# Attention's whole-array matmuls in one stretch, and its turned weights moved in 1280-byte pieces in a diagonal order

## The chip, the cores and the metric

The kernel runs on one core of a Trainium2 chip. The metric is the device time of one execution in microseconds (us). A core has five engines, each with a queue of its own that runs in order: TensorE (PE in the profile; its weight loads are PEld), VectorE (DVE), ScalarE (ACT), GpSimd (POOL) and SyncE, which here only issues DMA transfers (SPq). The transfers run on 16 DMA engines. SBUF is the on-chip memory of 128 partitions; PSUM holds the results of TensorE in 8 banks of 128x512 float32 numbers.

## The reference

The input x has 16 sequences of 512 tokens of width 256, all in float32. Three layers follow one another, each with a layer norm ahead and a residual around it: half a slot-and-expert layer, causal attention, and half a slot-and-expert layer again. The change is in attention alone:

```python
q = x @ Wq + bq;  k, v = split(x @ Wkv + bkv)   # 16 heads of 64
q, k = rope(q), rope(k)
probs = softmax(where(causal, q @ k.T / 8, -inf))
out = concat_heads(probs @ v) @ Wo + bo
x = x + out
```

## The kernel before

The first layer, attention and the last layer run one after another. Attention is cut into 64 units: each of the 16 sequences in 4 groups of 4 heads. A loop over u (from -2 to 63, near line 1100) runs one *turn* per step, and in a turn different units are at different stages: unit u has its weighted sums and output projection, unit u+1 its turning and its values, unit u+2 its scores and exponentials, unit u+3 its queries and keys. All engines run their instructions in the order in which the loop writes them out (manual_schedule), so the order of the lines is the order of each queue.

The stages, by the tile names in the profile:

- **p_av** (sums, L1054): probabilities times values, in tiles 128\*64 of the array, two heads side by side. It reads prT, the turned probabilities, and so waits for their transfers.
- **p_as** (scores, L956): queries times keys in tiles 32\*128, four heads at a time. A unit's rows come in four blocks: `scores((3,))` is the longest block of 512 columns; `scores((2,))` and `scores((1, 0))` are the others.
- **p_v** (values, L920), **p_q** and **p_k** (queries and keys, L898), **p_ay** (output projection, `leave`, L1070) and **p_ahT** (turning of a new sequence's x, `width`, L883, in every fourth turn) use the whole array, 128\*128.

After the scores VectorE adds the mask and takes the extremum (L974), ScalarE takes the exponential (L978), VectorE the reciprocal of the sum (L983), and GpSimd multiplies (L986, `scaled`). VectorE also rotates queries and keys (L904) with GpSimd (L909, L910), adds p_ay to x (L1076) and takes the statistics of finished tokens (`token_stats`, L198, L199).

The probabilities have to be turned (keys on partitions) for the sums. `turn_most`, `turn_corner` and `turn_rest` make seven VectorE transposes of 32x32 blocks into the tile sq (L1001). Then `move` (L1024) lets SyncE issue 16 transfers from sq to prT, each from one group of 32 partitions to another; both sides are 5120 contiguous bytes in each partition, and the outer loop is over the target group. The tiles sq and prT have one buffer each. PSUM's banks are handed out in turn: a new tile takes the bank of the tile eight before it, and waits until that has been read.

In a turn before, TensorE's order is p_av, (p_ahT), p_as of block 3, p_v, p_q, p_k, p_v, p_as of the other blocks, p_ay. `leave` returns a function, `added`, with p_ay's addition and the transfer of finished rows to memory; it is kept in the list `gone` and runs in the next turn, behind `move`. `spread` (ScalarE's square root for the layer norm) stands ahead of the second scores' exponentials, and `pair_rstd`, seven more square roots for the last layer, at the end of turn 60.

Of the kernel before, what the change touches and what calls it, by code (L numbers as in the profile page):

```python
# [9 lines left out]
F32 = mybir.dt.float32  # L10
AF = mybir.ActivationFunctionType
ALU = mybir.AluOpType
# [3 lines left out]
P = 128  # L16
NB, S, D = 16, 512, 256
# [3 lines left out]
PB = 2  # L21
# [13 lines left out]
HG = 4  # L35
NHG = AH // HG
SQ = 32
NSQ = P // SQ
# [9 lines left out]
def macaron_kernel(ctx: ExitStack, tc: tile.TileContext, a: dict, out: bass.AP):  # L48
# [144 lines left out]
    def token_stats(b, t):  # L193
        g = b // PB
        if b % PB == 0 and t == 0:
            mvs[g] = small.tile([P, PB * NT, 2], F32, tag=f"mv{g}", name=f"mv{g}", bufs=2)
        st = small.tile([P, 6], F32, tag="bnst", name=f"bnst{b}_{t}")
        nc.vector.bn_stats(st, xs[b][:, t, :])  # L198
        nc.vector.bn_aggr(mvs[g][:, (b % PB) * NT + t, :], st)  # L199
# [644 lines left out]
    def attention(qp, wq, wk, wv, wo, cos, sin, row):  # L844
# [14 lines left out]
        def scales(g, std):  # L859

            n = PB * NT
            rstds[g] = small.tile([P, n], F32, tag=f"rstd{g}", name=f"rstd{g}", bufs=1)
            nc.vector.reciprocal(rstds[g], std)
            pair_shift(g)
# [13 lines left out]
        def width(b):  # L878
            hTs[b] = qp.tile([P, NC, S], F32, tag="hT", name=f"ahT{b}", bufs=2)
            for c in range(NC):  # L880
                pt = ps(f"p_ahT{b}_{c}")
                for t in range(NT):
                    nc.tensor.transpose(pt[:, t * P:(t + 1) * P], hs[b][t // 2][:, t % 2, c * P:(c + 1) * P], ident)  # L883
                nc.scalar.copy(hTs[b][:, c, :], pt)  # L884
# [27 lines left out]
        def values(u, t0):  # L912
            b, hg = units[u]
            if t0 == 0:
                pool, tag, bufs = (ap, "v", 1) if u + 1 < nu else (qp, "hT", 2)
                vs[u] = pool.tile([P, NT, HG * DQ], F32, tag=tag, name=f"v{b}_{hg}", bufs=bufs)
            pv = ps(f"p_v{b}_{hg}_{t0}")
            for t in range(2):
                for k in range(NC):
                    nc.tensor.matmul(pv[:, t * 256:(t + 1) * 256], hTs[b][:, k, (t0 + t) * P:(t0 + t + 1) * P],  # L920
                                     wv[:, k, hg * HG * DQ:(hg + 1) * HG * DQ],
                                     start=(k == 0), stop=(k == NC - 1))
            nc.scalar.copy(vs[u][:, t0:t0 + 2, :].rearrange("p t d -> p (t d)"), pv)  # L923
# [8 lines left out]
        class Weights:  # L932
# [56 lines left out]
            def turn(self, which, heads, of, src, dst):  # L989

                if heads[0] == 0 and which == 0 and len(of) == 2:
                    self.sq = ap.tile([P, NSQ, HG, blocks * SQ], F32, tag="sq", name=f"sq{self.nm}")
                pr = self.pr[which]

                def view(x, at, dims):
                    return bass.AP(x.tensor, x.offset + at, [list(x.ap[0])] + [[s, n] for s, n in dims if n > 1])
                j, nh = heads
                step = (7, 3)[which] * P  # L1000
                nc.vector.transpose(  # L1001
                    view(self.sq, j * blocks * SQ + dst[0] * SQ,
                         [(blocks * SQ, nh)] + [(s * SQ, n) for s, (_, n) in zip(dst[1:], of)]
                         + [(HG * blocks * SQ, NSQ), (1, SQ)]),
                    view(pr, j * step + src * P,
                         [(step, nh)] + [(s * P, n) for s, n in of] + [(SQ, NSQ), (1, SQ)]))

# [10 lines left out]
            def move(self):  # L1018


                prT = prTs[self.u] = ap.tile([P, NSQ, HG, blocks * SQ], F32, tag="prT", name=f"prT{self.nm}")
                for k in range(NSQ):
                    for q in range(NSQ):
                        nc.sync.dma_start(prT[k * SQ:(k + 1) * SQ, q, :, :], self.sq[q * SQ:(q + 1) * SQ, k, :, :])  # L1024

            def turn_at_once(self):

# [37 lines left out]
        def leave(u, t0):  # L1065
            b, hg = units[u]
            py = ps(f"p_ay{b}_{hg}_{t0}")
            for t in range(2):
                for pair in range(HG // 2):
                    nc.tensor.matmul(py[:, t * D:(t + 1) * D], oTs[u][:, pair, (t0 + t) * P:(t0 + t + 1) * P],  # L1070
                                     wo[:, hg * (HG // 2) + pair, :],
                                     start=(pair == 0), stop=(pair == HG // 2 - 1))

            def added():
                xt = xs[b][:, t0:t0 + 2, :]
                nc.vector.tensor_tensor(xt, py.rearrange("p (t d) -> p t d", t=2), xt, ALU.add)  # L1076
                if hg == NHG - 1:
                    nc.sync.dma_start(xout[b][:, t0:t0 + 2, :], xt)
            return added

# [14 lines left out]
        seen = 2 * NHG  # L1097
        with tc.manual_schedule(engines={mybir.EngineType.DVE, mybir.EngineType.Activation,
                                         mybir.EngineType.Pool, mybir.EngineType.SP}):
            gone = []  # L1100
            for u in range(-2, nu):
                new = ws[u + 2] = Weights(u + 2) if u + 2 < nu else None
                qk = queries_keys(u + 3)
                old = ws.get(u + 1)
                fresh = u + 3 < nu and units[u + 3][1] == 0
                if fresh:
                    enter(units[u + 3][0])
                if u + 2 == nu:
                    old.scaled((1, 0))
                    values(u + 1, 0)  # L1110
                    values(u + 1, 2)
                if u >= 0:
                    sums(u, 0)
                    sums(u, 1)
                if old and u + 2 == nu:
                    old.turn_at_once()
                elif old:
                    old.turn_most(0)
                    old.scaled((1, 0), slice(0, HG // 2))
                    old.turn_most(1)  # L1120
                    old.scaled((1, 0), slice(HG // 2, HG))
                    old.turn_most(2)
                    old.turn_most(3)
                    old.turn_corner()
                    old.turn_rest()
                    old.move()
                for one in gone:
                    one()
                if fresh:
                    with_bias(units[u + 3][0])  # L1130
                if u + 4 in stds:
                    scales((u + 4) // (PB * NHG), stds.pop(u + 4))
                if fresh:
                    width(units[u + 3][0])
                if new:
                    new.scores((3,))
                    new.exps((3,))

                for at in range(seen, min(u + 13, NB * NHG)):
                    token_stats(*divmod(at, NHG))  # L1140
                seen = max(seen, u + 13)
                if u >= NHG + 1:
                    token_stats(*divmod(u - NHG - 1, NHG))
                if new:
                    new.scaled((3,))
                if 0 <= u + 1 < nu - 1:
                    values(u + 1, 0)
                for one in qk:
                    one()
                if 0 <= u + 1 < nu - 1:  # L1150
                    values(u + 1, 2)
                if 0 <= u + 5 < nu and (u + 5) % (PB * NHG) == 0:
                    stds[u + 5] = spread((u + 5) // (PB * NHG))
                if new:
                    new.scores((2,))
                    new.scores((1, 0))
                    new.exps((2,))
                    new.exps((1, 0), lambda: new.scaled((2,)))

                if u == nu - NHG:  # L1160
                    for g in range(NB // PB - 1):
                        pair_rstd(g)
                if u == nu - 1:
                    for g in range(PB):
                        entered[g] = xs[g]
                        for t in range(NT):
                            i = (g % PB) * NT + t
                            nc.vector.tensor_scalar(xs[g][:, t, :], xs[g][:, t, :], mvs[g // PB][:, i, 0:1],
                                                    rstds[g // PB][:, i:i + 1], ALU.subtract, ALU.mult)
                gone = [leave(u, 0), leave(u, 2)] if u >= 0 else []  # L1170
                if u >= nu - 2:
                    for one in gone:
                        one()
                    gone = []
            token_stats(NB - 2, NT - 1)
        yield
    with ExitStack() as es:
# [53 lines left out]
```

## Time and profile before

| what | us |
|---|---|
| median of 3 runs | 2330.49 |
| lowest and highest of the runs | 2329.22, 2330.73 |
| the profiled execution | 2332.58 |
| its span on the profile's page | 2330.9 |
| attention's first and last sums start (timeline of TensorE) | 447.5, 1937.2 |
| an ordinary turn, from p_av to p_av | 23.36 |

The page gives each engine's busy time and its share of the span. A timeline row gives start, duration, engine, line, operation, tiles and a count of merged instructions, and in brackets an idle time before it and what ended it. A tile's name carries its purpose: `p_av<-prT,v` writes p_av and reads prT and v. For matmuls the array tile is given (32\*128 is 32 rows by 128 columns). Each float32 matmul of the code appears as two records. A row of the windows view gives, for its stretch, each engine's busy time (and its number of instructions), the granted clock of TensorE, the busy share of the DMA engines and GB/s.

### The profile page before, as it was taken

The numbers are of one execution on the slowest core, as the hardware profiler recorded it, in microseconds if no ns is written. First come the engines' busy times: TensorE is split into PE (matmuls) and PEld (weight loads), VectorE is DVE, ScalarE is ACT, GpSimd is POOL, SyncE is SP. The second block draws the span as 40 slices with busy tenths as digits, with TensorE's granted clock in tenths as the row PEclk, the third lists the DMA queues.
The fourth block names the chain that finished last, engine by engine and source line by source line (L and its number), as shares of the span: only waits on it lengthen the run. The fifth ranks groups of instructions, "written<-read, shape, count | busy, mean of one in ns | idle before, by whom it ended". The sixth has DMA issues, their size and how long they took to land. (4 is left out here: it accounts for less than half of the span.)

```text
span 2330.9 us, 42260 instructions
## 1 busy us (share of the span) xinstructions
PE 2285.0 (98%) x14496; PEld 1453.5 (62%) x14496; DVE 1754.1 (75%) x4658; ACT 1123.7 (48%) x3046; POOL 1061.9 (46%) x1692
## 2 busy tenths in 40 slices
PE   7999999999999999999999999999999999999999
PEld 5665588465656565565656565655656566664588
DVE  6742397888888888898888888888888874442387
ACT  4743243455455545554645545554555454542233
POOL 2210054565555565655656555556565541210043
PEclk9999999999999999999999999999999999999999
DMA  6839851345555464645455555546464543839834
GB/s 223 252 124 406 321 137 46 85 97 129 107 119 126 103 134 93 142 103 129 107 123 113 126 111 116 129 100 137 91 140 105 127 110 96 241 115 405 329 115 140
DMA packets 159710, 346.77 MB, mean 149 GB/s; under 512 B 38980, under 2 KB 98952, under 8 KB 151304
## 3 DMA queue, kind: packets, MB, share of 16 engines
q1 hardware_dynamic: 158636, 343.27, 55.4%
q8 instruction: 115, 1.88, 0.4%
q14 instruction: 99, 0.81, 0.1%
q10 hardware_dynamic: 860, 0.81, 0.1%
HBM read 148.95 MB, written 29.88 MB: 77 GB/s over the span
## 5 line engine op out<-in xcount | busy, mean ns | idle before, releaser
L986 POOL TENSOR_SCALAR pr<-pr,ars 128x512 f32<-128x512 f32 (+3 forms) x1024 | 522.1, 532 | 631.5 <-DVE ars L983 631.5
L978 ACT ACTIVATE pr<-pr,amn 128x512 f32<-128x512 f32 (+3 forms) x1024 | 560.5, 549 | 268.4 <-DVE amn L974 268.2
L974 DVE CUSTOM_DVE_ANT_0 pr<-p_as,causal 128x512 f32<-128x512 f32 (+3 forms) x1024 | 433.9, 484 | 96.6 <-PE p_as L956 96.6
L1001 DVE STREAM_TRANSPOSE sq<-pr 128x768 f32<-128x768 f32 x441 | 379.0, 906 | 0.2 <-issue 0.2
L956 PE MATMUL p_as<-k,q 32*128 32x128 f32 (+3 forms) x4096 | 325.3, 445 | 7.1 <-DVE k L904 3.4
L1054 PE MATMUL p_av<-prT,v 128*64 128x512 f32 (+3 forms) x2048 | 292.1, 438 | 1.9 <-DVE amn L974 1.9
L956 PEld LDWEIGHTS p_as<-k,q 32*128 32x128 f32 x4096 | 192.4, 186 | 107.4 <-issue 49.6
L920 PEld LDWEIGHTS p_v<-wv,ahT 128*128 128x128 f32 x1024 | 189.4, 190 | 97.4 <-issue 75.6
L920 PE MATMUL p_v<-wv,ahT 128*128 128x256 f32 x1024 | 248.1, 385 | 0.0
L923 ACT COPY v<-p_v 128x512 f32<-128x512 f32 x128 | 73.3, 574 | 353.1 <-PE p_v L920 353.1
L1070 PE MATMUL p_ay<-wo,aoT 128*128 128x256 f32 x1024 | 240.5, 388 | 0.2 <-ACT aoT L1061 0.2
L1054 PEld LDWEIGHTS p_av<-prT,v 128*64 128x64 f32 x2048 | 138.1, 138 | 161.7 <-issue 136.5
L898 PE MATMUL p_k<-ahT,wk 128*128 128x512 f32 x512 | 230.6, 592 | 0.4 <-DVE amn L974 0.4
L898 PE MATMUL p_q<-ahT,wq 128*128 128x512 f32 x512 | 230.5, 593 | 0.2 <-ACT ahT L884 0.2
L1070 PEld LDWEIGHTS p_ay<-wo,aoT 128*128 128x128 f32 x1024 | 190.8, 191 | 32.0 <-ACT aoT L1061 0.6
L978 ACT ACTIVATION_READ_ACCUMULATOR pr<-pr,amn 128x1 f32 x1024 | 191.7, 187 | 0.0
L898 PEld LDWEIGHTS p_k<-ahT,wk 128*128 128x128 f32 x512 | 97.2, 190 | 122.7 <-issue 110.5
L898 PEld LDWEIGHTS p_q<-ahT,wq 128*128 128x128 f32 x512 | 97.1, 190 | 95.8 <-issue 85.4
L717 POOL TENSOR_TENSOR kbd<-kT,own 128x256 f32<-128x256 f32 x32 | 19.7, 619 | 267.4 <-DVE kT L680 235.5
L1061 ACT ACTIVATE aoT<-p_av,bcol 128x512 f32<-128x512 f32 x128 | 87.4, 684 | 108.9 <-PE p_av L1054 108.9
L770 PE MATMUL p_cy<-vw,catT 128*128 128x256 f32 x512 | 120.8, 379 | 0.0
L548 PE MATMUL p_ds<-hT,qk 128*128 128x512 f32 x256 | 118.3, 606 | 2.3 <-ACT hT L241 2.3
(167 smaller groups left out, 3252.0 us busy)
## 6 DMA issues: line engine op xcount, KB each, us to landing
prT<-sq SPq DMA_DIRECT2D x1008, 160.0 KB
w<-in_e_W_dram SPq DMA_DIRECT2D x64, 1024.0 KB
w<-in_e_Wg_dram SPq DMA_DIRECT2D x32, 1024.0 KB
out_dram<-x SPq DMA_DIRECT2D x64, 256.0 KB
awaya<-sqa SPq DMA_DIRECT2D x25, 512.0 KB
atT<-awaya SPq DMA_DIRECT2D x100, 128.0 KB
xl<-in_attn_x_dram SPq DMA_DIRECT2D x16, 512.0 KB
xl<-out_dram SPq DMA_DIRECT2D x16, 512.0 KB
```

Source lines behind the costliest of these rows:

```text
L548: nc.tensor.matmul(psc, qk[:, k, c * P:(c + 1) * P], hT[:, k, :], start=(k == 0), stop=(k == NC - 1))
L770: nc.tensor.matmul(py[:, t * D:(t + 1) * D], atT[:, c, t * P:(t + 1) * P], vws[b][:, c, :], start=(c == 0), stop=(c == NC - 1))
L898: nc.tensor.matmul(pq, self.w[:, k, at:at + P], hTs[self.b][:, k, :], start=(k == 0), stop=(k == NC - 1))
L920: nc.tensor.matmul(pv[:, t * 256:(t + 1) * 256], hTs[b][:, k, (t0 + t) * P:(t0 + t + 1) * P], wv[:, k, hg * HG * DQ:(hg + 1) * HG * DQ], s ...
L956: nc.tensor.matmul(banks[j][:, at:at + w], q[n][j * 32:(j + 1) * 32, i * P:(i + 1) * P], k[n][j * 32:(j + 1) * 32, :w], start=(n == 0), st ...
L974: nc.vector.tensor_tensor_reduce(out=self.at(i, j), in0=banks[j][:, at:at + w], in1=causal[:, S - w:], scale=-1.0 / math.sqrt(DQ), scalar= ...
L978: nc.scalar.activation(self.at(i, j), self.at(i, j), AF.Exp, bias=self.mn[:, i, j:j + 1], scale=-1.0, accum_out=self.rs[:, i, j:j + 1])
L986: nc.gpsimd.tensor_scalar(self.at(i, j), self.at(i, j), self.rs[:, i, j:j + 1], 1.0, ALU.mult, ALU.mult)
L1001: nc.vector.transpose(view(self.sq, j * blocks * SQ + dst[0] * SQ, [(blocks * SQ, nh)] + [(s * SQ, n) for s, (_, n) in zip(dst[1:], of)] + ...
L1054: nc.tensor.matmul(po[j * DQ:(j + 1) * DQ, :].rearrange("d (a f) -> d a f", a=NSQ)[:, :, t * SQ:], vs[u][:, t, head * DQ:(head + 1) * DQ], ...
L1061: nc.scalar.activation(oTs[u][:, pair, :].rearrange("d (i a y) -> d a i y", i=NT, a=NSQ), po.rearrange("d (a i y) -> d a i y", i=NT, a=NSQ ...
L1070: nc.tensor.matmul(py[:, t * D:(t + 1) * D], oTs[u][:, pair, (t0 + t) * P:(t0 + t + 1) * P], wo[:, hg * (HG // 2) + pair, :], start=(pair ...
```

## The change

The tile sq has its dimensions in another order, `[P, HG, NSQ, ...]` for `[P, NSQ, HG, ...]`, so that VectorE's transposes write the same 32-number runs to other places, and each transfer reads four pieces of 1280 bytes where it read one of 5120. The target side is as before. The order of the 16 transfers is diagonal: the target group k runs fastest, and the source group is (k + n) mod 4.

TensorE's order in a turn becomes p_av, p_as of block 3, p_v, (p_ahT), p_v, p_q, p_k, p_ay, p_as of the other blocks. `leave` makes its addition at once, and `gone` is no more. On ScalarE the copies of p_v stand ahead of the first scores' exponentials, and `spread` behind them. On GpSimd the rotations stand ahead of `scaled((3,))`, and the bias on x (`with_bias`) behind it. On VectorE the first scores' mask work follows `move`, then one token's statistics, the rotations, the additions of p_ay, another token's statistics, and the second scores. `pair_rstd` runs in turn 61, behind that turn's transposes. The counts and forms of the compute instructions are the same.

```diff
-                    self.sq = ap.tile([P, NSQ, HG, blocks * SQ], F32, tag="sq", ...)
+                    self.sq = ap.tile([P, HG, NSQ, blocks * SQ], F32, tag="sq", ...)
...
-                for k in range(NSQ):
-                    for q in range(NSQ):
-                        nc.sync.dma_start(prT[k * SQ:(k + 1) * SQ, q, :, :], self.sq[q * SQ:(q + 1) * SQ, k, :, :])
+                for n in range(NSQ):
+                    for k in range(NSQ):
+                        q = (k + n) % NSQ
+                        nc.sync.dma_start(prT[k * SQ:(k + 1) * SQ, q, :, :], self.sq[q * SQ:(q + 1) * SQ, :, k, :])
...
-            def added():
-                xt = xs[b][:, t0:t0 + 2, :]
-                nc.vector.tensor_tensor(xt, py..., xt, ALU.add)
-                if hg == NHG - 1:
-                    nc.sync.dma_start(xout[b][:, t0:t0 + 2, :], xt)
-            return added
+            xt = xs[b][:, t0:t0 + 2, :]
+            nc.vector.tensor_tensor(xt, py..., xt, ALU.add)
+            if hg == NHG - 1:
+                nc.sync.dma_start(xout[b][:, t0:t0 + 2, :], xt)
...
                     old.move()
-                for one in gone:
+                if u + 4 in stds:
+                    scales((u + 4) // (PB * NHG), stds.pop(u + 4))
+                if new:
+                    new.scores((3,))
+                if 0 <= u + 1 < nu - 1:
+                    values(u + 1, 0)
+                if fresh:
+                    width(units[u + 3][0])
+                if 0 <= u + 1 < nu - 1:
+                    values(u + 1, 2)
+                if new:
+                    new.exps((3,))
+                for one in stats:
+                    token_stats(*one)
+                for one in qk:
                     one()
+                if new:
+                    new.scaled((3,))
                 if fresh:
                     with_bias(units[u + 3][0])
-                if u + 4 in stds:
-                    scales((u + 4) // (PB * NHG), stds.pop(u + 4))
-                if fresh:
-                    width(units[u + 3][0])
-                if new:
-                    new.scores((3,))
-                    new.exps((3,))
...
-                if new:
-                    new.scaled((3,))
-                if 0 <= u + 1 < nu - 1:
-                    values(u + 1, 0)
-                for one in qk:
-                    one()
-                if 0 <= u + 1 < nu - 1:
-                    values(u + 1, 2)
                 if 0 <= u + 5 < nu and (u + 5) % (PB * NHG) == 0:
                     stds[u + 5] = spread((u + 5) // (PB * NHG))
-                if new:
-                    new.scores((2,))
-                    new.scores((1, 0))
-                    new.exps((2,))
-                    new.exps((1, 0), lambda: new.scaled((2,)))
-                if u == nu - NHG:
+                if u == nu - NHG + 1:
                     for g in range(NB // PB - 1):
                         pair_rstd(g)
...
-                gone = [leave(u, 0), leave(u, 2)] if u >= 0 else []
...
+                if u >= 0:
+                    leave(u, 0)
+                    leave(u, 2)
+                for one in left:
+                    token_stats(*one)
+                if new:
+                    new.scores((2,))
+                    new.scores((1, 0))
+                    new.exps((2,))
+                    new.exps((1, 0), lambda: new.scaled((2,)))
```

More of the change, by code (lines that the diff above doesn't have):

```diff
@@ L993, in turn @@
                 if heads[0] == 0 and which == 0 and len(of) == 2:
-                    self.sq = ap.tile([P, NSQ, HG, blocks * SQ], F32, tag="sq", name=f"sq{self.nm}")
+                    self.sq = ap.tile([P, HG, NSQ, blocks * SQ], F32, tag="sq", name=f"sq{self.nm}")
                 pr = self.pr[which]
@@ L1001, in turn @@
                 nc.vector.transpose(
-                    view(self.sq, j * blocks * SQ + dst[0] * SQ,
-                         [(blocks * SQ, nh)] + [(s * SQ, n) for s, (_, n) in zip(dst[1:], of)]
-                         + [(HG * blocks * SQ, NSQ), (1, SQ)]),
+                    view(self.sq, j * NSQ * blocks * SQ + dst[0] * SQ,
+                         [(NSQ * blocks * SQ, nh)] + [(s * SQ, n) for s, (_, n) in zip(dst[1:], of)]
+                         + [(blocks * SQ, NSQ), (1, SQ)]),
                     view(pr, j * step + src * P,
@@ L1072, in leave @@
                                      start=(pair == 0), stop=(pair == HG // 2 - 1))
-            def added():
-                xt = xs[b][:, t0:t0 + 2, :]
-                nc.vector.tensor_tensor(xt, py.rearrange("p (t d) -> p t d", t=2), xt, ALU.add)
-                if hg == NHG - 1:
-                    nc.sync.dma_start(xout[b][:, t0:t0 + 2, :], xt)
-            return added
+            xt = xs[b][:, t0:t0 + 2, :]
+            nc.vector.tensor_tensor(xt, py.rearrange("p (t d) -> p t d", t=2), xt, ALU.add)
+            if hg == NHG - 1:
+                nc.sync.dma_start(xout[b][:, t0:t0 + 2, :], xt)
         def queries_keys(u):
@@ L1099, in attention @@
                                          mybir.EngineType.Pool, mybir.EngineType.SP}):
-            gone = []
             for u in range(-2, nu):
@@ L1105, in attention @@
                 fresh = u + 3 < nu and units[u + 3][1] == 0
+                stats = [divmod(at, NHG) for at in range(seen, min(u + 13, NB * NHG))]
+                seen = max(seen, u + 13)
+                left = [divmod(u - NHG - 1, NHG)] if u >= NHG + 1 else []
                 if fresh:
@@ L1126, in attention @@
                     old.move()
-                for one in gone:
+                if u + 4 in stds:
[13 more added lines that the diff above has]
+                for one in qk:
                     one()
+                if new:
+                    new.scaled((3,))
                 if fresh:
                     with_bias(units[u + 3][0])
-                if u + 4 in stds:
-                    scales((u + 4) // (PB * NHG), stds.pop(u + 4))
-                if fresh:
-                    width(units[u + 3][0])
-                if new:
-                    new.scores((3,))
-                    new.exps((3,))
[L1139 to L1143, printed above, removed]
-                if new:
-                    new.scaled((3,))
-                if 0 <= u + 1 < nu - 1:
-                    values(u + 1, 0)
-                for one in qk:
-                    one()
-                if 0 <= u + 1 < nu - 1:
-                    values(u + 1, 2)
                 if 0 <= u + 5 < nu and (u + 5) % (PB * NHG) == 0:
                     stds[u + 5] = spread((u + 5) // (PB * NHG))
-                if new:
-                    new.scores((2,))
-                    new.scores((1, 0))
-                    new.exps((2,))
-                    new.exps((1, 0), lambda: new.scaled((2,)))
-                if u == nu - NHG:
+                if u == nu - NHG + 1:
                     for g in range(NB // PB - 1):
@@ L1169, in attention @@
                                                     rstds[g // PB][:, i:i + 1], ALU.subtract, ALU.mult)
-                gone = [leave(u, 0), leave(u, 2)] if u >= 0 else []
[L1171 to L1174, printed above, removed]
+                if u >= 0:
[8 more added lines that the diff above has]
+                    new.exps((1, 0), lambda: new.scaled((2,)))
             token_stats(NB - 2, NT - 1)
```

## The prediction

> **What bounds the kernel now.** I read the first part of the page, then the timeline of TensorE (PE) over one turn of attention, then the timelines of VectorE (DVE) and of the DMA queue (SPq) in the same turn, then the windows of one microsecond for the bytes moved.
>
> ```profile
> PE 2285.0 (98%) x14496; PEld 1453.5 (62%) x14496; DVE 1754.1 (75%) x4658; ACT 1123.7 (48%) x3046; POOL 1061.9 (46%) x1692
> ```
>
> TensorE is busy nearly always, so a change gains by what it takes from TensorE and loses by each wait that it puts there. The timeline of one turn (start, duration, line, tiles):
>
> ```profile
> 995.28 4.53 PE L1054 MATMUL p_av<-prT,v 128*64 128x512 f32 x32
> 999.74 2.00 PE L956 MATMUL p_as<-k,q 32*128 32x512 f32 x16
> 1001.66 1.99 PE L920 MATMUL p_v<-wv,ahT 128*128 128x256 f32 x8
> 1003.50 3.60 PE L898 MATMUL p_q<-ahT,wq 128*128 128x512 f32 x8
> 1006.93 3.60 PE L898 MATMUL p_k<-ahT,wk 128*128 128x512 f32 x8
> 1010.36 1.89 PE L920 MATMUL p_v<-wv,ahT 128*128 128x256 f32 x8
> 1012.18 2.88 PE L956 MATMUL p_as<-k,q 32*128 32x384 f32 x48
> 1014.99 3.72 PE L1070 MATMUL p_ay<-wo,aoT 128*128 128x256 f32 x16
> 1018.64 0.65 PE L1054 MATMUL p_av<-prT,v 128*64 128x512 f32 x2
> ```
>
> No row shows an idle time, and the turn is 1018.64 - 995.28 = 23.36 us; 62 turns have this set of stages. By the starts the stages take 4.46, 1.92, 1.84, 3.43, 3.43, 1.82, 2.81 and 3.65 us. The turn's transfers (16, from SPq) and the work before them:
>
> ```profile
> 1001.34 10.80 SPq L1024 DMA_DIRECT2D prT<-sq  x16
> ```
>
> ```profile
> 1013.77 0.56 DVE L974 CUSTOM_DVE_ANT_0 pr<-p_as,causal 128x384 f32<-128x384 f32 x1 [1.44 <-PE p_as L956]
> ...
> 1018.09 0.97 DVE L1001 STREAM_TRANSPOSE sq<-pr 128x768 f32<-128x768 f32 x1
> ...
> 1020.51 4.12 DVE L1001 STREAM_TRANSPOSE sq<-pr 128x768 f32<-128x768 f32 x5
> 1024.55 0.65 DVE L1076 TENSOR_TENSOR x<-p_ay,x 128x512 f32<-128x512 f32 x1
> ```
>
> ```profile
> 1002.00:1003.00 1.00, 1.00 (x6) 0.90 (x5) 1.00 (x4) 0.00 (x0) 0.00 (x0) 1.00 0.68 138
> 1008.00:1009.00 1.00, 1.00 (x3) 0.38 (x2) 1.00 (x3) 0.00 (x0) 1.00 (x2) 1.00 0.97 205
> 1014.00:1015.00 1.00, 1.00 (x29) 0.85 (x21) 1.00 (x5) 0.63 (x3) 0.00 (x0) 1.00 0.64 123
> ```
>
> The last two numbers of a window are the busy share of the DMA engines and GB/s: bytes flow from 1002.5 to about 1015 at some 200 GB/s. By their completion marks the last of the 16 lands 14.46 us after the first issue (the usual turn), at 1015.8; the sums that read them start at 1018.64. So **2.8 us are spare**, and that is the cover which the change spends.
>
> **The change part by part.** Sums are against the profiled execution, 2332.58 us (span 2330.9 and 1.7 around it). The median of the runs is 2330.49, so 2.1 come off at the end.
>
> *Fewer changes of tile shape on TensorE.* Consecutive matmuls of one shape start 0.216 us apart at 256 columns, 0.429 at 512. At a change between the whole array (128\*128) and tiles (32\*128, 128\*64) more is paid: the last matmul of p_v is followed after 0.309 instead of 0.216 (0.094), the second matmul of p_ay after 0.320 (0.104). Before, a turn goes sums, scores, whole array, scores, whole array (p_ay), sums; after, p_ay stands with p_v, p_q, p_k, and one exit from the whole array and one entry go: 0.198 us. What comes anew, scores directly to sums, no row shows. Its nearest rows are sums to scores (0.20 in all) and the two halves already paid, the end of the scores (0.108) and the first of the sums (0.05); I take these halves, as they are the same stages. Bounds of the saving: 0.14 to 0.36 us a turn. 62 x 0.198 = **-12.3** (-9 to -22).
> In 15 turns the turning of x (p_ahT) stands between sums and scores and costs 1.02 us for 8 matmuls of 0.109; after, it stands inside the whole-array stretch: 15 x 0.145 = **-2.2**.
>
> *Two stalls.* In 7 turns the second scores take 3.44 instead of 2.81: ScalarE's (ACT) square root falls just before the exponentials there and makes VectorE late. After, it comes behind the first exponentials, about 13 us into the turn, and ScalarE next has work at 22: 7 x 0.63 = **-4.4** (0 if it isn't hidden).
> The seven square roots at the end of attention (pair_rstd) now stand ahead of the transposes of turn 61:
>
> ```profile
> 1898.24 0.59 DVE L204 RECIPROCAL rstd<-std_g 128x8 f32<-128x8 f32 x3 [3.86 <-ACT std_g L203]
> ```
>
> That turn is 29.95 us where its stages sum to 20.05. After, they stand behind the transposes of that turn, so the transfers no longer wait for them; sums are then due about 24 us into it. I take **-5.5** (0 to -9.9).
>
> *VectorE, later against TensorE.* Its work is the same. Call S the start of the second scores. Before and after, VectorE begins their exponentials at S+1.59, the transposes at S+5.91 (1018.09 - 1012.18), and SPq issues the first transfer at S+12.52 (1024.70). Before, the next sums start at S+6.46; after, at S+2.81, since p_ay no longer lies between. So transposes and transfers start 3.65 us later against the sums. Queued on VectorE ahead of S+1.59 are now the additions of p_ay and one token's statistics: p_ay's end at S+0.18, 0.59 for the addition, 0.55 for the statistics, S+1.32: 0.27 us early. GpSimd (POOL): scaling by 1/sum of the first scores moves behind the rotations, done at S+2.6; the next scaling is due at S+4.8. In the 15 turns its 2.8 us for the bias lie between, until S+5.4, and the first head's scaling (0.55) then ends when its transpose is due. PSUM's 8 banks: the tightest is the last bank of the second scores, which waits for the addition of p_ay at S+0.8 and is wanted at S+1.4. None of these is late by the rows, by small margins.
>
> *The deadline of the transfers.* From S, the next turn's sums come at S+2.81, the next S 20.35 later (4.46+1.92+1.84+1.73+6.86+3.45+0.09), and the sums that read the transfers 2.81 after that: S+25.97. Less the issue at S+12.52 and 0.05 for the wait, **13.4 us** are allowed; today's 14.46 is too long. One lap of this chain is two turns, so each us above 13.4 costs 0.5 a turn, 31 in all.
>
> *How long the transfers take after.* 16 transfers of 160 KB land 0.81 us apart, whatever partitions they read. Two intervals alone are shorter, 0.71 and 0.75: there the target changes from partitions 32 to 63 to 64 to 95. Changes 31 to 32 and 95 to 96 save nothing. So crossing partition 64 saves 0.16. Before crosses once; the diagonal order (targets 0, 32, 64, 96, 0 ...) crosses 7 times: 14.46 - 6 x 0.16 = **13.5 us**. Lower bound: SPq's issue, 15 x 0.635 us, and 2.47 to the first landing: 12.0. Upper bound: no saving, and the price of pieces. No row shows 1280 bytes; packets of 1024 take 0.046 and of 2048 0.084 (medians), so four of 1280 take about 0.222 against 0.194 for the fastest of 5120, and with 32 rows an engine at most 0.9 us: 15.35. While engines contend (a row then takes 0.40) that price should hide; I take 0. SPq's issue is no bound: 128-piece transfers (atT) issue every 0.475 us.
> A rule speaks against my 0.16. The Trainium skill, "SBUF — State Buffer", section "Can I just issue two DMAs to hit both halves?", says that they serialize, and gives +6% for two transfers to partitions 0 and 64. By it the 12.9 us of data would be 12.2, the transfers 13.7 us and the end 7 us later than my forecast; the rows above neither confirm nor refute it, since they show one crossing in each turn.
> At 13.5 the cost is 31 x 0.09 = **+2.8**.
>
> *The sum.* 2332.6 - 12.3 - 2.2 - 4.4 - 5.5 + 2.8 = 2311.0; less 2.1, **2309 us** (-0.9%).
>
> **The rivals.**
> *Transfers become the bound (slower).* If the order saves nothing, they take 14.46 us, 1.06 over: +33 in place of +2.8, 2339 us; with the full price of the pieces 1.95 over, 2366. The place is the first p_av of a turn, waiting for DMA prT. It decides from 14.0 us: 2306 + 31 x 0.64 = 2326 is 0.2% under the median; from 14.35 us the kernel is slower. For it: the steady 0.81 at every other interval. Against it: the two short ones.
> *The order saves half.* 13.9 us: 2306 + 15 = 2321.
> *TensorE gains nothing by the stretch.* Going from scores to sums could cost as much as what goes (the lower bound and more): 2309 + 12 = 2321. Against it, both halves are in the trace.
> *VectorE late at S+1.59.* Each 0.1 us late adds 3 us by the same chain; 0.5 late gives 2325.
>
> **How the numbers follow.** Transfers of at most 13.6 us, near 2309: 0.40. The middle cases, 2314 to 2325: 0.16. Within 0.2% (2326 to 2335; about what a measurement of this kernel can tell from no change): 0.12. Slower, 2336 to 2366: 0.32, of which 0.14 above 2350. Faster is 0.56. Low end: transfers in time and the larger savings of the bounds, 2306 - 10 = 2296; I set 2300. High end 2350. The likeliest case's own range is 2300 to 2314.
>
> **What would show it.** Right: p_av starts 23.2 us apart in plain turns; p_ay directly after p_k with 0.43 between its neighbours and no extra 0.2; the second scores never 3.44 long; the last landing at most 13.5 us after the first issue; no wait before p_av. Wrong: rows of p_av with an idle time from DMA prT, with plain turns near 23.7; landing intervals of 0.81 throughout or more; VectorE busy past S+1.6 with p_ay's additions.

## The result, and the profile after

The changed kernel takes **2354.26 us** (median of 4 runs, 2351.47 to 2357.35) beside 2329.85 us for the kernel before (4 runs, 2328.36 to 2330.73): a ratio of 1.0102, with a 95% interval of 1.0090 to 1.0114. It is slower by 1%, where 2309 us were forecast. The profiled execution took 2357.35 us, with a span of 2355.6.

From the page of the changed kernel: TensorE's row, the row of the DMA queue that carries the transfers (packets, MB, share of 16 engines), and the group of the sums, whose last column is the idle time just before them.

```profile
PE 2266.0 (96%) x14496; PEld 1468.5 (62%) x14496; DVE 1765.3 (75%) x4658; ACT 1115.0 (47%) x3046; POOL 1066.8 (45%) x1692
...
q1 hardware_dynamic: 255404, 343.27, 57.5%
...
L1055 PE MATMUL p_av<-prT,v 128*64 128x512 f32 (+3 forms) x2048 | 293.5, 439 | 49.8 <-DVE amn L974 39.9
```

The same two rows of the kernel before:

```profile
q1 hardware_dynamic: 158636, 343.27, 55.4%
...
L1054 PE MATMUL p_av<-prT,v 128*64 128x512 f32 (+3 forms) x2048 | 292.1, 438 | 1.9 <-DVE amn L974 1.9
```

TensorE has 19 us less to do (2285.0 before), so the stretch gives something. The idle time in front of the sums has grown from 1.9 to 49.8 us, which is more. The timeline of TensorE over two turns of the changed kernel shows where:

```profile
1002.64 4.53 PE L1055 MATMUL p_av<-prT,v 128*64 128x512 f32 x32 [1.70 <-DVE amn L974]
1007.10 2.00 PE L956 MATMUL p_as<-k,q 32*128 32x512 f32 x16
1009.03 3.72 PE L920 MATMUL p_v<-wv,ahT 128*128 128x256 f32 x16
1012.59 3.60 PE L898 MATMUL p_q<-ahT,wq 128*128 128x512 f32 x8
1016.02 3.60 PE L898 MATMUL p_k<-ahT,wk 128*128 128x512 f32 x8
1019.45 3.62 PE L1071 MATMUL p_ay<-wo,aoT 128*128 128x256 f32 x16
1023.00 2.88 PE L956 MATMUL p_as<-k,q 32*128 32x384 f32 x48
1025.94 4.53 PE L1055 MATMUL p_av<-prT,v 128*64 128x512 f32 x32
...
1046.30 2.88 PE L956 MATMUL p_as<-k,q 32*128 32x384 f32 x48
1050.61 0.65 PE L1055 MATMUL p_av<-prT,v 128*64 128x512 f32 x2 [1.43 <-DVE amn L974]
```

Inside the turn nothing waits, and p_ay follows p_k without an extra step. The first row and the last begin with idle times of 1.70 and 1.43 us; the turn between has hardly any. The row names an instruction of VectorE, but that had long been done: a wait for several semaphores is put down to the one that came last in the profile, and here it was a DMA. SPq's row shows the transfers of the last wait:

```profile
1035.52 10.33 SPq L1025 DMA_DIRECT2D prT<-sq  x16
```

They are issued 12.52 us after the second scores' start at 1023.00, as before. By the completion marks the last lands at 1050.20, 14.68 us after the first issue, and the sums start at 1050.61. Without the wait they would have started at 1049.11 (1046.30 and 2.81).

### The profile page after: what moved, and what is told of

It is laid out like the page before. It is cut to its first block, busy times and chain, and to the rows that moved or that the text cites. A ratio compares the mean times of both kernels' runs of the same rounds, so it can differ in the third digit from the quotient of the medians.

```text
span 2355.6 us, 42292 instructions
## 1 busy us (share of the span) xinstructions
PE 2266.0 (96%) x14496; PEld 1468.5 (62%) x14496; DVE 1765.3 (75%) x4658; ACT 1115.0 (47%) x3046; POOL 1066.8 (45%) x1692
## 5 line engine op out<-in xcount | busy, mean ns | idle before, releaser
L1055 PE MATMUL p_av<-prT,v 128*64 128x512 f32 (+3 forms) x2048 | 293.5, 439 | 49.8 <-DVE amn L974 39.9
L956 PE MATMUL p_as<-k,q 32*128 32x128 f32 (+3 forms) x4096 | 318.2, 443 | 3.7 <-DVE k L904 2.0
L909 POOL TENSOR_TENSOR q<-q,q 128x512 f32<-128x512 f32 x64 | 81.4, 1272 | 499.4 <-DVE q L904 499.4
L1055 PEld LDWEIGHTS p_av<-prT,v 128*64 128x64 f32 x2048 | 152.9, 138 | 185.8 <-issue 97.5
L920 PE MATMUL p_v<-wv,ahT 128*128 128x256 f32 x1024 | 242.5, 388 | 0.0
L1071 PE MATMUL p_ay<-wo,aoT 128*128 128x256 f32 x1024 | 231.8, 379 | 0.2 <-ACT aoT L1062 0.2
L1075 DVE TENSOR_TENSOR x<-p_ay,x 128x512 f32<-128x512 f32 x128 | 88.3, 691 | 79.7 <-PE p_ay L1071 79.7
L904 DVE SCALAR_TENSOR_TENSOR q<-p_q,bcol,cos 128x512 f32<-128x512 f32 x128 | 94.6, 739 | 42.1 <-PE p_q L898 41.9
```

The costliest lines, as they stand in the source:

```text
L904: nc.vector.scalar_tensor_tensor(m, pq, bcol[:, r:r + 1], tab, ALU.add, ALU.mult)
L909: nc.gpsimd.tensor_tensor(self.halves[0], self.m[0, 0], self.m[1, 0], ALU.subtract)
L956: nc.tensor.matmul(banks[j][:, at:at + w], q[n][j * 32:(j + 1) * 32, i * P:(i + 1) * P], k[n][j * 32:(j + 1) * 32, :w], start=(n == 0), st ...
L1055: nc.tensor.matmul(po[j * DQ:(j + 1) * DQ, :].rearrange("d (a f) -> d a f", a=NSQ)[:, :, t * SQ:], vs[u][:, t, head * DQ:(head + 1) * DQ], ...
```

## The experiments

In the tables, "transfers" is the time from the first issue to the last landing (median of 63 units), and "waits" is how much later than 2.81 us after the second scores' start the sums begin, added up over turns 1 to 60. (The page's idle time in front of the sums also counts the first and the last units, and leaves out some 0.07 us of each wait, under the modelled end of the scores.) Ratios are to the kernel before on the same chip.

**The form of the transfers, taken apart.** Four kernels: the kernel before with the new transfers, and the changed kernel with the other three combinations of order and piece.

The kernel before with the new form of both `sq` and the loop:

> The kernel before, with the transfers alone in the new form (pieces of 1280 bytes, diagonal order). Theory "deadline": the transfers take as long as before (14.5 to 14.8 us), and the 2.8 us that are spare before hide any small difference, so 2330 +- 3 us with the last landing 14.5 to 14.8 us after the first issue. Rival "the new form costs by itself" (contention with other traffic, VectorE's transposes slower for their new target): 2336 us or more.

The changed kernel with the old form of both:

> The changed kernel with the transfers of before (5120 bytes, target by target). Theory "deadline": a time of 14.5 us is still 1.1 us too long, and the slope of 31 us for each us of the transfers gives 2354 less 31 x 0.1 to 0.2, so 2348 to 2352 us, with a wait in front of p_av in every second turn. Rival "pieces": if the 1280 bytes make the wait, it goes, and the time is 2310 to 2325. Rival "the stretch itself costs" (VectorE late, changes of tile shape): 2354, with the last landing ahead of p_av.

Pieces of 5120 bytes in the diagonal order:

```diff
-   self.sq = ap.tile([P, HG, NSQ, blocks * SQ], F32, tag="sq", ...)
+   self.sq = ap.tile([P, NSQ, HG, blocks * SQ], F32, tag="sq", ...)
...
-   nc.sync.dma_start(prT[k * SQ:(k + 1) * SQ, q, :, :], self.sq[q * SQ:(q + 1) * SQ, :, k, :])
+   nc.sync.dma_start(prT[k * SQ:(k + 1) * SQ, q, :, :], self.sq[q * SQ:(q + 1) * SQ, k, :, :])
```

> The changed kernel with its diagonal order but pieces of 5120 bytes. It parts order from pieces. My prediction's step (0.16 us saved at each of 7 crossings of partition 64, pieces free) would give 13.5 us and 2309 to 2315 here if only the pieces spoilt it. Theory "deadline, and the order buys nothing": landings 0.8 us apart, 14.3 to 14.6 us in all, 2345 to 2352 us.

Pieces of 1280 bytes, target by target:

```diff
-   for n in range(NSQ):
-       for k in range(NSQ):
-           q = (k + n) % NSQ
+   for k in range(NSQ):
+       for q in range(NSQ):
```

> The changed kernel with pieces of 1280 bytes in the old order, target by target. Theory "deadline, order and pieces worth little": 2352 to 2362 us, last landing 14.6 to 15.0. Rival "the diagonal order costs": below 2345. If the order had saved about 0.3 us hidden under the price of the pieces, 2364 or more.

| TensorE's order | order of transfers | piece | transfers, us | waits, us | time, us | ratio |
|---|---|---|---|---|---|---|
| before | by target | 5120 | 14.50 | 0 | 2330.8 | 1 |
| before | diagonal | 1280 | 14.68 | 0 | 2330.5 | 0.9999 (0.9991 to 1.0008) |
| after | by target | 5120 | 14.52 | 42.5 | 2348.8 | 1.0082 (1.0069 to 1.0096) |
| after | diagonal | 1280 | 14.64 | 46.7 | 2354.3 | 1.0102 (1.0090 to 1.0114) |
| after | diagonal | 5120 | 13.67 | 17.8 | 2326.2 | 0.9979 (0.9970 to 0.9987) |
| after | by target | 1280 | 15.37 | 66.0 | 2398.9 | 1.0291 (1.0277 to 1.0305) |

The diagonal order and the small pieces both count, with opposite signs. The order takes 0.85 us off the transfers with pieces of 5120 bytes and 0.73 with 1280; the pieces add 0.97 in the diagonal order and 0.85 in the other. Together they leave 0.1, so the change as a whole looked like one that does nothing to the transfers, which is what I expected of all four kernels. That the order buys nothing and that the pieces cost nothing were both wrong: the first two expectations held, the third missed at both of its values, and the fourth came out far above its middle case, on the side of an order that saves something hidden under the price of the pieces. With the old order of TensorE the two together change nothing: their 0.2 us lie within its 2.8 us of spare time.

The groups of the sums tell the same in one column (pieces of 5120 in the diagonal order, then of 1280 target by target):

```profile
L1055 PE MATMUL p_av<-prT,v 128*64 128x512 f32 (+3 forms) x2048 | 292.2, 438 | 18.8 <-DVE amn L974 12.3
```

```profile
L1054 PE MATMUL p_av<-prT,v 128*64 128x512 f32 (+3 forms) x2048 | 315.2, 464 | 71.7 <-DVE amn L974 33.1
```

Idle time falls to 18.8 us in the one and rises to 71.7 in the other. In the other the sums themselves are slower too, 464 ns in the mean in place of 438; that is taken up below.

**Fewer transfers.** Four of the 16 transfers go from a group of 32 partitions to the same group; ScalarE can copy these where it is idle.

```diff
 for n in range(NSQ):
     for k in range(NSQ):
         q = (k + n) % NSQ
+        if n == 0 and k < 4:
+            continue
         nc.sync.dma_start(...)
...
+def stay(self):
+    for k in range(4):
+        nc.scalar.copy(prTs[self.u][k * SQ:(k + 1) * SQ, k, :, :], self.sq[k * SQ:(k + 1) * SQ, :, k, :])
...
     new.exps((3,))
+if old and u + 2 < nu:
+    old.stay()
```

> The changed kernel with 12 transfers a turn in place of 16: the four from a group of 32 partitions to the same group are copies by ScalarE (32x1280 each), behind the exponentials of the first scores, where ScalarE is idle from about 13 to 22 us into a turn. Theory "deadline": the last landing comes 4 x 0.79 us earlier, 11.4 us after the first issue, less than the 13.4 allowed; no wait at p_av, plain turns 23.17 us, and the stretch pays what the prediction had for it: 2354 less 46, so 2305 to 2312 us. Rival "the stretch itself costs": turns stay at 23.7 in the mean and the time above 2335. Rival "ScalarE becomes late": the copies take over 9 us and the second scores' exponentials wait, 2320 to 2340.

With two copies and 14 transfers:

> As the run with 12 transfers, with 14 transfers and two copies: one point on the way. Theory "deadline": last landing about 13.0 to 13.2 us after the first issue, 0.2 to 0.4 below the allowed 13.4, less the 0.35 us from landing to p_av, so the waits almost go: 2308 to 2320 us. If the deadline were 12 us or less, 2325 to 2340.

The same four copies in the kernel before:

> The kernel before with 12 transfers and four copies by ScalarE. Theory "deadline": the kernel before is bound by TensorE and its transfers had 2.8 us to spare, so shorter ones bring nothing: 2330 +- 4 us. Rival "fewer transfers make any of these kernels faster" (less traffic, SBUF contention): 2320 or less.

And the same bytes in four wide transfers, `prT[:, k, :, :] <- sq[:, :, k, :]`, a kernel that leaves out the exchange between the groups of partitions:

> The changed kernel with the same bytes in 4 transfers over all 128 partitions each, and no exchange between the groups of partitions (that part of the turning is left out). It asks whether the 0.8 us for 160 KB is a limit of the bytes or of the 32 partitions. If of the bytes: last landing 13.5 to 14.5 us after the first issue and 2340 to 2352 us. If of the 32 partitions or of the issues: 4 to 10 us, no wait at p_av, 2305 to 2312 us.

| kernel | transfers, us | waits, us | time, us | ratio |
|---|---|---|---|---|
| after, 14 transfers | 13.11 | 5.8 | 2315.7 | 0.9938 (0.9926 to 0.9951) |
| after, 12 transfers | 11.09 | 0 | 2309.7 | 0.9911 (0.9896 to 0.9926) |
| after, 4 wide transfers | 9.26 | 0 | 2302.8 | 0.9880 (0.9866 to 0.9893) |
| before, 12 transfers | 11.16 | 0 | 2343.3 | 1.0054 (1.0042 to 1.0067) |

With transfers of 13.11 us the waits are nearly gone, with 11.09 us they are, and TensorE's new order is worth what it was forecast to be worth. So the stretch itself costs nothing, which removes that rival. The wide transfers narrow down what makes 160 KB take 0.8 us. In windows of the wide transfers (the last two numbers are the busy share of the DMA engines and GB/s):

```profile
1016.00:1017.00 1.00, 1.00 (x4) 0.52 (x3) 1.00 (x5) 1.00 (x5) 0.00 (x0) 1.00 1.03 355
1017.00:1018.00 1.00, 1.00 (x4) 0.43 (x3) 0.97 (x4) 1.00 (x3) 0.00 (x0) 1.00 1.03 358
```

355 GB/s with all 128 partitions at once, against some 210 with 32 and the same pieces (160 KB every 0.78 us). The issues don't make the difference: SPq issues every 0.65 us, faster than the landings come. So the bytes alone aren't the limit. It comes with the narrow transfers; but the wide ones have 128 partitions for 32 and also 640 KB for 160, and no run here takes these two apart. The busy share of the DMA engines, about 1 in both, doesn't show the limit.

The kernel before with 12 transfers missed its expectation by 13 us, for reasons of my own making. One is seen in ScalarE's rows there:

```profile
1127.65 5.05 ACT L1030 COPY prT<-sq 32x1280 f32<-32x1280 f32 x4
1132.72 1.07 ACT L923 COPY v<-p_v 128x512 f32<-128x512 f32 x2
```

In that kernel the copies of p_v come behind the new copies in ScalarE's queue, and PSUM's banks come free late:

```profile
1133.36 2.86 PE L956 MATMUL p_as<-k,q 32*128 32x384 f32 x42 [0.33 <-ACT v L923]
```

But this makes the second scores only 4.2 us longer in 60 turns. The first scores are 12.5 us longer, all in the turns with a new sequence (3.05 or 2.44 us in place of 1.93); attention starts 4.2 us earlier there, which takes back a part. There one of the weight loads of the scores waits for the addition of p_ay:

```profile
857.76 0.31 PEld L956 LDWEIGHTS p_as<-k,q 32*128 32x128 f32 x8 [0.84 <-DVE x L1082]
```

The addition comes no later than before, at 5.9 us after the sums' start in both kernels; there the scores didn't have to wait for it. Why they do here I have not traced. The run tells nothing of the transfers. That the kernel before has nothing to gain from shorter ones rests on its zero waits and on the first run of the table above.

**The square roots alone.** In the kernel before, `spread` goes ahead of the queries and keys, and `pair_rstd` a turn later:

```diff
+if 0 <= u + 5 < nu and (u + 5) % (PB * NHG) == 0:
+    stds[u + 5] = spread((u + 5) // (PB * NHG))
 for one in qk:
     one()
...
-if 0 <= u + 5 < nu and (u + 5) % (PB * NHG) == 0:
-    stds[u + 5] = spread((u + 5) // (PB * NHG))
+if u == nu - NHG + 1:
+    for g in range(NB // PB - 1):
+        pair_rstd(g)
 if new:
     new.scores((2,))
...
-if u == nu - NHG:
-    for g in range(NB // PB - 1):
-        pair_rstd(g)
```

> The kernel before with only its square roots moved: spread between the copies of p_v, pair_rstd a turn later behind the transposes. It measures two terms of the prediction alone, 4.4 us for the seven stalls of the second scores and 5.5 us (0 to 9.9) for the turn with 29.95 us: 2320 to 2323 us. If the square roots merely make something else late (the second copy of p_v), 2326 to 2331.

It took 2321.05 us beside 2331.36, a ratio of 0.9955 (0.9941 to 0.9969): 10.3 us, where the two terms said 9.9. In its trace none of the second scores is 3.44 us long any more (7 were), and turn 61 takes 24.03 us in place of 29.95.

**A better version.** The run with 12 transfers lost 6.6 us in turn 61 (31.11 us, where this version takes 24.55): there the copies stood ahead of the seven square roots on ScalarE. So: 12 transfers, pieces of 5120 bytes, and all 16 transfers for that one unit.

```diff
+self.whole = self.u == nu - 2
+for n in range(0 if self.whole else 1, NSQ):
     for k in range(NSQ):
         q = (k + n) % NSQ
         nc.sync.dma_start(prT[k * SQ:(k + 1) * SQ, q, :, :], self.sq[q * SQ:(q + 1) * SQ, k, :, :])
```

> The version that the runs so far point to: the changed kernel with 12 transfers of 5120-byte pieces in the diagonal order and four copies by ScalarE, but all 16 transfers in the last turn that has any, where the copies stood ahead of the seven square roots and made the second scores wait (12.07 us in place of 7.12). Last landing about 10.5 us after the first issue, no wait at p_av, and 5 to 6 us less in that turn than the run with 12 transfers: 2302 to 2306 us. If the 2310 us of that run had another cause than its tail: 2308 to 2311.

It takes **2302.09 us** beside 2331.36, a ratio of 0.9878 (0.9864 to 0.9891), with transfers of 10.53 us. From its page, the copies that took the place of a quarter of the transfers, and the sums:

```profile
L1030 ACT COPY prT<-sq 32x1280 f32<-32x1280 f32 x248 | 310.6, 1252 | 2.2
L1060 PE MATMUL p_av<-prT,v 128*64 128x512 f32 (+3 forms) x2048 | 291.3, 437 | 1.3 <-DVE amn L974 1.3
```

ScalarE has 311 us more to do, and TensorE's idle time in front of the sums is gone.

**Slow sums behind long waits.** In the kernel with 1280-byte pieces target by target, 13 of the 60 sums take about 6.15 us in place of 4.46. The windows around one of them (the number ahead of the DMA's share is TensorE's granted clock):

```profile
1168.10:1170.70 2.60, 0.00 (x0) 0.00 (x1) 2.57 (x18) 2.60 (x12) 0.49 (x1) 1.00 0.30 52
1170.70:1172.70 2.00, 1.97 (x9) 0.88 (x11) 2.00 (x7) 2.00 (x10) 2.00 (x5) 0.77 0.01 4
1172.70:1174.70 2.00, 2.00 (x12) 1.33 (x10) 1.57 (x4) 2.00 (x7) 2.00 (x6) 0.50 0.00 0
1174.70:1176.90 2.20, 2.20 (x20) 1.20 (x16) 2.20 (x3) 1.25 (x3) 1.01 (x3) 0.89 0.00 0
1176.90:1178.80 1.90, 1.90 (x18) 0.69 (x16) 0.76 (x2) 0.69 (x1) 0.00 (x0) 1.00 0.00 0
```

TensorE stands still for 2.6 us; then the clock falls to 0.50, at 1171.8 us, and 3.4 us later it is full again. To test whether the wait does it, small matmuls that compute nothing that is kept were put in front of the sums:

```diff
 po = ps(f"p_av{b}_{hg}_{pair}")
+for n in range(10 if pair == 0 else 0):
+    nc.tensor.matmul(po[:DQ, :P], ident[:, :DQ], ident, start=True, stop=True)
```

> The changed kernel with 1280-byte pieces target by target (2398.9 us), with ten small matmuls ahead of the first sums of a unit that compute nothing that is kept, 1.1 us of work on TensorE before the wait. In that kernel 13 of the sums took 6.15 us in place of 4.46, with a granted clock of 0.69 to 0.82, all behind waits of over 2 us: 21.9 us in all. Theory "a long wait lowers the granted clock": the work shortens the waits without moving the deadline, the clock stays up, and the time falls to 2374 to 2388 although TensorE has 66 us more to do. Rival "those sums are slow for another reason" (reading prT just behind the transfers): 2398 or more.

It took 2445.68 us (1.0492, 1.0478 to 1.0506), and so speaks for the rival by the letter. But I had priced the filling at half: its row reads

```profile
1034.57 2.29 PE L1051 MATMUL p_av<-ident 128*64 128x128 f32 x19
```

and that is 2.17 us a turn with its last record, more than the waits held. So TensorE became the bound. With five:

> As the run before, with five of the matmuls in place of ten. Each float32 matmul is two records of 0.108 us, so ten were 2.17 us a turn and not 1.1: they filled every wait and more, and TensorE became the bound at 25.34 us a turn. Five are 1.08 us, a little less than the mean wait of 1.10 us a turn in the kernel without them. Theory "a long wait lowers the granted clock": no sums of 6.15 us, and a turn falls from 24.86 us in the mean to 24.5 to 24.7, so 2377 to 2389 us with 67 us of work added. Rival "those sums are slow for another reason": 2398 or more.

It took **2381.31 us** (1.0218, 1.0204 to 1.0232). That is 17.6 us less than without the filling, with 67 us of useless work added. Its group of the sums:

```profile
L1056 PE MATMUL p_av<-prT,v 128*64 128x512 f32 (+3 forms) x2048 | 296.9, 436 | 3.5 <-DMA prT<-sq 2.3
```

The mean of a sum is back at 436 ns, and the waits that are left have their right name, the DMA. Between 460 and 1960 us the granted clock doesn't fall once. So the wait does lower the clock.

## Why the prediction was wrong

**The step that failed** is the time of the transfers, and in it one term: the price of pieces of 1280 bytes. The prediction set 0.9 us as its upper bound and took 0: "While engines contend (a row then takes 0.40) that price should hide; I take 0." It doesn't hide: 0.97 us in the diagonal order, 0.85 in the other. In the diagonal order the first landing comes 2.64 us after the first issue in place of 2.48, and the intervals behind it are some 0.05 longer (0.75 and 0.80 in turn, against 0.70 and 0.74). With the prediction's own 31 us for each us, this term alone is 31 x 0.97 = 30 us, and 2309 becomes 2339. Three smaller ones make up the rest: the order (0.11 us less than forecast, 3 us), the step from the landing to the sums (below, 7 us), and the units with a late landing, which lift the mean from the median's 14.64 to 14.77 us (4 us). Together 2353, where 2354 was measured; part of that agreement is luck, since the waits came out somewhat smaller than 31 us for each us, turn 61 gained less, and attention began 2.6 us earlier, which was not forecast.

**The order of the transfers** was forecast to save 0.96 us and saved 0.85 (0.73 with the small pieces): right in sign and nearly in size, for a reason that the traces bear out only in a small part. I expected 7 short intervals where the target crosses partition 64. With pieces of 5120 bytes those are 0.70 us and the others 0.74, so crossing saves 0.04 and not 0.16 (0.05 with small pieces); the rest is that from the third on all intervals are shorter than the usual 0.81. That the size came out nearly right is luck. The Trainium skill, "SBUF — State Buffer", section "Can I just issue two DMAs to hit both halves?", which the prediction weighed against its own figure, did better: the estimate from its 6% was 13.7 us, and the run with 5120-byte pieces shows 13.67.

**From the landing to the sums** I allowed 0.05 us; in the changed kernel the 35 units that wait show 0.13 to 0.46, 0.27 in the mean. That is the 7 us.

**The deadline** held: 13.4 us allowed, and half of the excess a turn. By it the waits would be 31 x (14.77 + 0.27 - 0.05 - 13.4) = 49 us for the changed kernel (14.77 is the mean of the transfers), and 20, 46 and 71 us for the kernels of 13.67, 14.52 and 15.37 us, with their means and delays. Measured are 46.7, and 17.8, 42.5 and 66.0: 5 to 9% less, which could come from the 0.87 us that every fourth turn has to spare by its p_ahT (31 x 0.22 = 7 us at most); that was not tested. The lap of two turns is in the timeline above: one turn waits, the next doesn't.

**TensorE's own gain** held. Plain turns without a wait take 23.17 us, fresh ones 24.04, as 0.198 and 0.145 us said. The seven stalls are gone. Turn 61 gains 5.4 us in the best version (5.5 forecast) and 3.8 in the changed kernel, where it still waits. Not forecast: the first sums of attention start at 441.1 us in the best version, in place of 447.5, and at 444.9 in the changed kernel.

**The rivals.** The time fell to "transfers become the bound", and it acts at the place named, the first p_av of a turn. But I had it as an order that saves nothing, and gave it 2339 us; it was an order that saves and pieces that cost. VectorE was not late, and the change from scores to sums costs no more than assumed: both would show in the runs without waits, which are at 23.17 us a turn. Summed up in the profiled executions, from the kernel with four wide transfers (span 2300.4) to the changed one (2355.6) there are 55.2 us: 46.7 of waits and 1.7 of one slow sum in the 60 turns, 3.4 before the second unit's sums start, 1.5 in turn 61, and 1.9 that I have not placed.

## What to carry to other kernels

When a change spends a cover, the row that was hidden under it has to be priced to a tenth of a us, each part by itself: here one edit took 0.85 us off the transfers and its companion put 0.97 back, and in the old order of the work the pair could not be seen. A bound taken from a row, such as 0.9 us for the pieces, is the estimate until a row shows that something hides it. And where a transfer is the bound, look first for the part of it that needn't be a transfer: four local copies on an idle engine took 3.55 us off the transfers (14.64 to 11.09), where their order took 0.73 to 0.85.

## What the hardware showed that I had not expected

- TensorE's clock falls behind waits of 2 us. In the kernel above 13 of 60 sums ran at a granted clock down to 0.50, behind idle times of 1.97 to 2.77 us, and paid 1.7 us each; idle times of up to 2.55 us went by without it. The trace tells the two apart. Its stretches at 0.50 behind these waits are 3.41 us long and start whole multiples of 3.413 us apart (670.03, 721.23, 772.43, 823.63 us: 15 of them each time). Laid on that grid, the 30 waits of over 1 us in turns 1 to 61 sort by the idle time that falls into one cell: with 2.06 us or more the next cell is at 0.50 in 12 of 12, with 1.95 or less in none of 13, with 1.97 to 2.02 in 2 of 5. A wait that is cut in two by the grid goes free, as 2.43 us do here (two cells with 1.95 and 0.48 us idle), and the one of 2.63 us doesn't (1168.38, 2.35 us idle):

```profile
1018.19:1021.61 3.42, 1.47 (x36) 1.23 (x28) 3.21 (x18) 2.64 (x9) 1.32 (x2) 1.00 0.74 126
1021.61:1025.02 3.41, 2.93 (x20) 1.65 (x22) 2.98 (x13) 3.41 (x17) 3.24 (x7) 1.00 0.00 0
1168.38:1171.79 3.41, 1.06 (x6) 0.57 (x8) 3.38 (x20) 3.41 (x15) 1.58 (x3) 1.00 0.15 27
1171.79:1175.21 3.42, 3.42 (x17) 1.94 (x14) 2.99 (x6) 3.42 (x12) 3.42 (x9) 0.50 0.00 0
```

The changed kernel agrees: of its waits in turns 1 to 61 one alone puts over 1.9 us into a cell (2.14 us), and behind it alone the clock falls. The Trainium skill, "TensorE: Matmul & The Clock Gate", section "What's actually happening", puts the fall at one idle window of about 3.4 us; the length agrees, but here 2 us of idle time in it are enough. So the price of the transfers is no straight line: 29 us for each us from 13.67 to 14.64, and 61 from 14.64 to 15.37.
- Small pieces cost between SBUF and SBUF. The Trainium skill, "DMA: Bandwidth & Descriptors", section "Why small descriptors are slow (HBM only)", says that such transfers don't suffer the penalty of small descriptors; here pieces of 1280 bytes made them 6 to 7% longer than pieces of 5120. The measurement decides.
- In the kernels with 16 transfers a fifth to a quarter of the units have late landings, and transfers 0.4 to 1.1 us longer than the median (13 of 63 in the kernel before, 15 after). The turn that the prediction shows is one of them: its last completion mark comes at 1016.22 us and not at 1015.8, since from the 11th transfer on one of the 16 marks of each trails the other 15, by up to 1.2 us. What delays them was not tried, and neither was which side of a transfer, source or target, makes the diagonal order faster.
